# Layer 2's attention: exponentials one piece later, weighting ahead of scores, side work dealt by a piece's width, expert choice from an image's second chunk

## The chip, the core and the metric

The kernel runs on one core of a Trainium2 chip, as one program. The metric is the device time of one execution in microseconds (us). Before the change three runs took 7749.14, 7749.23 and 7750.11 us: the median is 7749.23.

The core's engines run their own queues in order: PE (TensorE; PEld is its weight load), DVE (VectorE), ACT (ScalarE), POOL (GpSimd) and SP, which issues the DMA transfers. They wait for each other by semaphores.

## What is computed

Four layers in a row act on an image batch of 4 x 56 x 56 x 128 in float32. Only layer 2 is touched. An image is seen there as 3136 tokens of 128 channels; first comes attention with additive scores, then a mixture of 64 experts in which each expert chooses 8 tokens:

```
h = x.shape[-1]
f = einsum('bih,ha->bia', x, W1[:h]);  g = einsum('bjh,ha->bja', x, W1[h:])      # 16 features
t = tanh(f[:, :, None, :] + g[:, None, :, :] + b1)
scores = einsum('bija,a->bij', t, w2[:, 0]) + b2[0]
e = exp(scores) * tril(ones, -1)                     # query i sees keys j < i
out = einsum('bij,bjh->bih', e / (sum(e) + 1e-10), x)
...
probs = softmax(x @ gate_w.T + gate_b, over tokens)  # each of 64 experts takes its 8 best tokens,
...                                                  # pools them, runs two matrix products with gelu
outputs.at[chosen tokens].add(expert output * its share)
```

Every pair of tokens (query after key) costs 16 tanh, and these are most of the layer's work.

## The kernel before, in words

**Pieces.** `layer2_attention` (L1007) cuts an image's 28 tiles of 112 tokens into four *chunks* of seven query tiles (784 queries). For chunk k, keys come in tiles J = 0 to 7(k + 1) - 1, and each key tile in two halves. A (chunk, J, half) is a *piece*; all four images make 560 of them (`pieces`, L1042 on). `span` (L1046) gives the queries that a piece needs: all 784 while J lies before the chunk, and in the chunk's last seven key tiles 784, 728, 672 and so on down to 56, as later keys are seen by fewer queries. The first kind is called *wide* here, the end of a chunk *narrow*. An image's first chunk has narrow pieces only.

**A piece's own work.** `adds` (L1157): seven VectorE adds of a query feature tile and a key scalar into a tile `th` (three buffers). `tangents` (L1169): one tanh over all seven on ScalarE. `scores` (L1175): 28 matmuls, or 14 where only one half of the columns is left, that sum the 16 features into a PSUM tile `s` (two buffers, one for both halves of a J). For each J then `weights` (L1196): one or two exponentials on ScalarE into `e` (two buffers), and in a chunk's last seven key tiles a triangular mask on GpSimd (L1208); and `weighted` (L1210): two or four matmuls of `e` and the keys into the PSUM tile `o` (one buffer per chunk).

**Order.** The stage is scheduled by hand: the order in which the Python loop (L1283 on) calls these functions is the order in each engine's queue. For piece i the loop calls the tanh of i; then `deal(0)`; then the adds of piece i + 2; the scores of i; after those, in a first half the exponential of the key tile before, in a second half its weighting; then `deal(1)`.

**Side work** is cut into small steps in four lists, and each `deal` (L1268) takes at most one step: from `urgent`, else from `now`, else (only in `deal(1)`) from `later_on`, else from `behind`. A step issues its instructions at once and can leave a rest (most often a copy out of PSUM on VectorE), which the next `deal` issues first. `urgent` and `now` get what a finished chunk needs (`attended`, L1223: two copies of `o`, then four `added` steps that divide and add to X) and the twelve steps that prepare the next chunk (`chunk_steps`, L1074: norm, transpose (`turn`), `by_group` with a GpSimd memset and eight DMA transfers into `xk`, `keys`, `queries`, each for four and for three tiles). `later_on` gets the next image's statistics and first chunk. `behind` gets the expert choice of the image before (`choose_steps`, L1388: statistics L1402, a square root through `rstd`, norms, transposes, logits, then over 3136 columns a maximum L1442, an exponential L1446, shares L1450, the best eight L1454 and their replacement L1459, then places and pooling), from J = 2 of each image's first chunk on; and in the last image the experts themselves for images 0 to 2 (`experts2_steps`, L1507: 32 weight loads of 1 MB, narrow, multiply, gelu; then per image a matrix by expert L1602, its copy L1610, and seven pairs of `scatter` L1616 and `scattered` L1622 that add to X). A step marked as holding the PSUM tile `m` keeps the other lists waiting for one deal.

Before the first adds of a chunk, `add_ahead` (L1258) runs whatever is left of `now` and `later_on` in line, each step with its rest at once. After the last piece, L1323 runs what is left of all lists in the same way, and only then does layer 3 (L1649) begin, with statistics of image 0 (L1828, L1829).

Of the kernel before, what the change touches and what calls it, by code (L numbers as in the profile page):

```python
# [18 lines left out]
B, HW, C = 4, 56, 128  # L19
S = HW * HW  # L20
P = 128
TP = 2 * HW
# [23 lines left out]

WT = 7
HALF = WT * TP // 2

E2, H2, K2 = 64, 512, 8  # L50
NHC = H2 // P
# [59 lines left out]
class Hybrid:  # L111
# [895 lines left out]
    def layer2_attention(self):  # L1007
# [5 lines left out]
        with ExitStack() as ctx:  # L1013
# [17 lines left out]
            pools = self.f2_wide, self.f2_sm, m, hold  # L1031
            root = lambda var: self.rstd(sm, var, [TP, NT], 1e-5, "ln", bufs=1)
# [4 lines left out]
            chunks = [(t, min(WT, NT - t)) for t in range(0, NT, WT)]  # L1037
            order = [(b, k) for b in range(B) for k in range(len(chunks))]


            pieces = [
                (j, J, half)  # L1042
                for j, (b, k) in enumerate(order) for J in range(sum(chunks[k])) for half in range(2)
            ]

            def span(j, J, half=0):  # L1046

                t, n = chunks[order[j][1]]
# [101 lines left out]
            def rounds(half):  # L1150

                return [
                    [(blk, 2 * half + q) for blk in range(3)] + ([(3, half)] if q == 0 else [])
                    for q in range(2)
                ]
# [13 lines left out]
            def tangents(i):  # L1169
                j, J, half = pieces[i]  # L1170
                lo, hi = span(j, J, half)
                own = th[i][:, :, lo:hi]
                nc.scalar.activation(own, own, AF.Tanh)  # L1173

            def scores(i):  # L1175
                j, J, half = pieces[i]
                if half == 0:
                    ps[j, J] = self.t(ps_s, [P, 2, 512], "s")
                z = th.pop(i)
                after = [h for h, _, _ in halves(*span(j, J, 1))]  # L1180
                at = 0
                for n, groups in enumerate(rounds(half)):
                    for h, lo, hi in halves(*span(j, J, half)):
                        for s, (blk, q) in enumerate(groups):
                            off = QW - JG - JG * q
                            rows = min(QW, TP - QW * blk)
                            nc.tensor.matmul(  # L1187
                                ps[j, J][QW * blk : QW * blk + rows, h, lo:hi],
                                place[:, off : off + rows],
                                z[:, at + s, h * HALF + lo : h * HALF + hi],  # L1190
                                start=(half == 0 and n == 0),
                                stop=(n == 1 or blk == 3) and (half == 1 or h not in after),
                            )
                    at += len(groups)

            def weights(j, J):  # L1196
                e = es[j, J] = self.t(sm, [TP, WT * TP], "e")
                s = ps.pop((j, J))[:TP, :, :HALF]
                lo = span(j, J)[0]
                if lo == 0:  # L1200
                    nc.scalar.activation(e.rearrange("p (h q) -> p h q", h=2), s, AF.Exp, bias=b2)  # L1201
                else:
                    for h, at, end in halves(*span(j, J)):
                        nc.scalar.activation(
                            e[:, h * HALF + at : h * HALF + end], s[:, h, at:end], AF.Exp, bias=b2
                        )
                if J >= chunks[order[j][1]][0]:
                    nc.gpsimd.tensor_mul(e[:, lo : lo + TP], e[:, lo : lo + TP], later)  # L1208

            def weighted(j, J):  # L1210
                b, k = order[j]
                t, n = chunks[k]
                if J == 0:
                    po[j] = self.t(ps_o, [P, 2, 512], "o")
                e = es.pop((j, J))
                for h, lo, hi in halves(*span(j, J)):
                    nc.tensor.matmul(  # L1217
                        po[j][:, h, lo:hi], xk[b, J // WT][:, J % WT, :],
                        e[:, h * HALF + lo : h * HALF + hi],
                        start=(J == 0), stop=(J == t + ((h + 1) * HALF - 1) // TP),  # L1220
                    )

            def attended(j):  # L1223
                b, k = order[j]
                t, n = chunks[k]
                oT = {}

                def copied(h):
                    if h == 0:
                        oT[0] = self.t(sm, [P, WT * TP], "oT", bufs=1)  # L1230
                    nc.vector.tensor_copy(oT[0][:, h * HALF : (h + 1) * HALF], po[j][:, h, :HALF])

                def added(s):
                    return self.attended_tiles(
                        b, t + s, min(2, n - s), oT[0][:, s * TP :], 1e-10, back, sm, ps_m, "m"
                    )

                return [bind(copied, h) for h in range(2)], [bind(added, s) for s in range(0, n, 2)]
# [11 lines left out]
                run(step)  # L1250
            weights2 = lambda: setattr(self, "w2", self.experts2_weights(self.f2_w, m))
            urgent, now, later_on, behind = [], [], [], []
            state = SimpleNamespace(held=False, after=lambda: None)
            first = {}
            for i, (j, J, _) in enumerate(pieces):
                first.setdefault(j, i)
# [1 line left out]
            def add_ahead(i):  # L1258
                if i < len(pieces):
                    j = pieces[i][0]  # L1260
                    if i == first[j] and j:
                        while now or later_on:
                            assert not state.held
                            run((now or later_on).pop(0))
                    adds(i)


            def deal(odd):  # L1268
                state.after()
                step = None  # L1270
                if urgent and not state.held:
                    step = urgent.pop(0)
                elif now and not state.held:
                    step = now.pop(0)
                elif later_on and odd and not state.held:
                    step = later_on.pop(0)
                elif behind:
                    step = behind.pop(0)
                    state.held = step.holds
                state.after = (step and step()) or (lambda: None)  # L1280

            add_ahead(0)
            add_ahead(1)  # L1283
            for i, (j, J, half) in enumerate(pieces):
                tangents(i)
                b, k = order[j]
                if half == 0 and J == 1 and k + 1 < len(chunks):
                    now += chunk_steps(j + 1)
                    if j == 0:
                        now.append(weights2)  # L1290
                if half == 0 and J == 8 and k + 1 == len(chunks) and b + 1 < B:
                    assert not behind
                    later_on += image_steps(b + 1) + chunk_steps(j + 1)
                if half == 0 and J == 2 and k == 0 and b:


                    behind += self.choose_steps(
                        b - 1, self.f2_pooled[:, :, b - 1], self.w2, pools, root
                    )
                    if b == B - 1:  # L1300
                        behind += self.experts2_steps(
                            range(B - 1), self.f2_pooled, self.w2, pools, 3, lambda: None
                        )
                deal(0)
                add_ahead(i + 2)
                scores(i)
                before = pieces[i - 2][:2] if i >= 2 else None
                if before and half == 0:
                    weights(*before)
                if before and half == 1:  # L1310
                    assert J != 1 or not urgent or j == 0
                    weighted(*before)
                    if before[0] != j:
                        copied, added = attended(before[0])
                        urgent += copied
                        now += added
                deal(1)
            state.after()
            j, J, _ = pieces[-1]
            weights(j, J)  # L1320
            weighted(j, J)
            copied, added = attended(j)
# [657 lines left out]
```

## Time and profile before

| | |
|---|---|
| median of three runs | 7749.23 us |
| the profiled execution | 7740.81 us |
| its span, first to last instruction | 7738.9 us |
| mean granted TensorE clock | 0.942 |
| busy over the span | PE 6639.4, DVE 6034.2, ACT 4865.4, POOL 2636.1 us |
| layer 2's attention, first to last tanh (L1173) | 3559.3 to 6192.5 us |
| tanh on ACT, L1173 | x560, 2181.6 us |
| adds on DVE, L1164 | x3920, 1866.2 us |
| scores on PE, L1187 | x14112, 1419.6 us |
| weighting on PE, L1217 | x1024, 390.7 us |
| exponentials on ACT, L1201 and L1204, in this stage | 167.8 and 63.1 us |
| mask on POOL, L1208 | x112, 144.1 us (half of them under 0.5 us each) |

How to read what follows. A row of a timeline has the start, the time from the first to the last of the instructions that it merges, the engine, line, operation, and what is written and read; in brackets stands how long the engine had been idle and who ended it. A wait row has who waited for whom, the sum in us, how often, and the longest. A row of the table by stages has a stretch of time and the busy time of each engine in it, with the number of instructions, then the granted clock (1.00 is full speed), the busy share of the DMA engines and GB/s. Matmul ends are modelled and spans on POOL are rough.

### The profile page before, as it was taken

The numbers are of one execution on the slowest core, as the hardware profiler recorded it, in microseconds if no ns is written. First come the engines' busy times: TensorE is split into PE (matmuls) and PEld (weight loads), VectorE is DVE, ScalarE is ACT, GpSimd is POOL, SyncE is SP. The second block draws the span as 40 slices with busy tenths as digits, with TensorE's granted clock in tenths as the row PEclk, the third lists the DMA queues.
The fourth block names the chain that finished last, engine by engine and source line by source line (L and its number), as shares of the span: only waits on it lengthen the run. The fifth ranks groups of instructions, "written<-read, shape, count | busy, mean of one in ns | idle before, by whom it ended". The sixth has DMA issues, their size and how long they took to land.

```text
span 7738.9 us, 105360 instructions
## 1 busy us (share of the span) xinstructions
PE 6639.4 (86%) x41289; PEld 2755.4 (36%) x41289; DVE 6034.2 (78%) x10279; ACT 4865.4 (63%) x4329; POOL 2636.1 (34%) x1938
## 2 busy tenths in 40 slices
PE   7888998999899899987777777777688889999999
PEld 3442333333333333323223332332233344454544
DVE  5786999999999999998787877888788754444434
ACT  4454556555655555556998899899899933333332
POOL 4555777777777777772001000100101100000000
PEclk9998999999999999998998999899899989999999
DMA  3000000000000000000000000000003201210000
GB/s 64 6 2 1 1 1 1 1 1 1 1 1 1 1 1 1 1 1 11 3 1 5 5 6 3 5 7 1 5 5 115 80 8 60 89 48 5 5 5 6
DMA packets 93641, 108.76 MB, mean 14 GB/s; under 512 B 24952, under 2 KB 56790, under 8 KB 92631
## 3 DMA queue, kind: packets, MB, share of 16 engines
q1 hardware_dynamic: 93143, 102.02, 4.6%
q8 instruction: 325, 5.32, 0.3%
q14 instruction: 173, 1.42, 0.1%
HBM read 85.28 MB, written 10.29 MB: 12 GB/s over the span
## 4 chain that ended last, share of the span: by engine, by line
PE 35%; DVE 34%; ACT 20%; issue 7%; POOL 2%; DVEq 0%; DMA 0%; SPq 0%; ACTq 0%; POOLq 0%
DVE hs L765 16%; ACT th L1173 12%; PE o L1761 7%; PE q L1750 7%; DVE u L758 6%; PE s L1187 5%; DVE th L1164 5%; PE pe L1915 2%; PE a L728 2%; DVE e L493 2%; ACT E L753 2%; PE m L894 2%; PE o L1217 1%; ACT e L1201 1%; DVE d L528 1%
## 5 line engine op out<-in xcount | busy, mean ns | idle before, releaser
L1173 ACT ACTIVATE th<-th 128x5488 f32<-128x5488 f32 (+13 forms) x560 | 2181.6, 3932 | 131.7 <-DVE th L1164 117.6
L770 POOL TENSOR_TENSOR hs<-hs,bc 128x896 f32<-128x896 f32 x896 | 1867.1, 2084 | 787.9 <-DVE hs L765 765.7
L1164 DVE TENSOR_SCALAR th<-fT,g 128x784 f32<-128x784 f32 (+13 forms) x3920 | 1866.2, 548 | 323.9 <-PE s L1187 271.1
L765 DVE TENSOR_TENSOR_SCAN hs<-E,u 128x896 f32<-128x896 f32 x896 | 1810.0, 2020 | 117.9 <-ACT E L753 2.0
L1187 PE MATMUL s<-th,place 128*32 128x392 f32 (+7 forms) x14112 | 1419.6, 497 | 489.2 <-ACT th L1173 487.4
L753 ACT ACTIVATE E<-a 128x896 f32<-128x896 f32 x896 | 821.5, 917 | 803.9 <-PE u L737 334.4
L728 PE MATMUL a<-delta,A_pick 32*128 32x448 f32 x3584 | 982.5, 600 | 143.8 <-ACT E L753 135.6
L758 DVE TENSOR_TENSOR u<-u,bc 128x896 f32<-128x896 f32 x896 | 964.1, 1076 | 60.0 <-PE u L737 59.5
L737 PE MATMUL u<-du,pick 32*128 32x448 f32 x3584 | 974.6, 600 | 35.2 <-DVE hs L765 35.2
L1187 PEld LDWEIGHTS s<-th,place 128*32 128x32 f32 (+1 forms) x14112 | 463.6, 113 | 1348.8 <-ACT th L1173 689.7
L1755 ACT ACTIVATE e<-q,shift 128x448 f32<-128x448 f32 (+1 forms) x700 | 441.4, 633 | 750.6 <-PE q L1750 750.4
L1761 PE MATMUL o<-e,xk 128*128 128x448 f32 (+1 forms) x1400 | 654.9, 550 | 25.7 <-ACT oT L1736 25.7
L1920 DVE SCALAR_TENSOR_TENSOR X<-pe,r_gate,X 112x128 f32<-112x128 f32 x896 | 314.1, 351 | 454.3 <-PE pe L1915 418.5
L1750 PE MATMUL q<-xT 128*128 128x448 f32 (+1 forms) x1400 | 654.0, 549 | 2.3 <-ACT e L1755 2.2
L728 PEld LDWEIGHTS a<-delta,A_pick 32*128 32x128 f32 x3584 | 295.4, 188 | 691.7 <-ACT E L753 467.7
L1208 POOL TENSOR_TENSOR e<-e,later 112x112 f32<-112x112 f32 x112 | 144.1, 1289 | 1140.2 <-ACT e L1201 658.9
L1217 PE MATMUL o<-e,xk 112*128 112x392 f32 (+5 forms) x1024 | 390.7, 501 | 75.1 <-POOL e L1208 75.1
L776 PE MATMUL y<-hs,sum 128*32 128x448 f32 x3584 | 446.4, 569 | 4.4 <-POOL hs L770 4.4
L1104 POOL MEMSET xa<- 112x4 f32 (+1 forms) x32 | 19.8, 619 | 1055.8 <-PE m L1097 1055.8
L1761 PEld LDWEIGHTS o<-e,xk 128*128 128x128 f32 (+1 forms) x1400 | 263.0, 192 | 310.5 <-issue 275.5
L737 PEld LDWEIGHTS u<-du,pick 32*128 32x128 f32 x3584 | 295.2, 188 | 197.6 <-DVE hs L765 181.5
L1750 PEld LDWEIGHTS q<-xT 128*128 128x128 f32 (+1 forms) x1400 | 248.9, 189 | 239.0 <-issue 213.8
(262 smaller groups left out, 7255.8 us busy)
## 6 DMA issues: line engine op xcount, KB each, us to landing
wide<-in_L_ffn_weight SPq DMA_DIRECT2D x64, 1024.0 KB
X<-in_x SPq DMA_DIRECT2D x8, 784.0 KB
out<-X SPq DMA_DIRECT2D x28, 224.0 KB
M<-wide SPq DMA_DIRECT2D x4, 784.0 KB
wide<-M SPq DMA_DIRECT2D x4, 784.0 KB
xk<-xa SPq DMA_DIRECT2D x96, 32.0 KB
xk<-xa SPq DMA_DIRECT2D x96, 24.0 KB
e_edge<-dtab SPq DMA_DIRECT2D x42, 49.0 KB
```

The source lines that it names most:

```text
L728: nc.tensor.matmul(halves(to)[:, k], w["A"][own, order[j][2], f, q, :], pre[j]["delta"][own, f], start=True, stop=True,)
L737: nc.tensor.matmul(halves(to)[:, k], w["pick"][own, q, :], pre[j]["du"][own, f], start=True, stop=True,)
L753: nc.scalar.activation(E[p + 1], t, AF.Exp)
L758: nc.vector.tensor_mul(v, v, pre[p // PAIRS]["bc"][:, 0:1].to_broadcast([P, 2, CH]))
L765: nc.vector.tensor_tensor_scan(flat, E.pop(p), V.pop(p), 0.0, op0=ALU.mult, op1=ALU.add)
L770: nc.gpsimd.tensor_mul(HS[p], HS[p], bc[:, 1:2].to_broadcast([P, 2, CH]))
L1164: nc.vector.tensor_scalar(th[i][:, s, lo:hi], fT[j][:, lo:hi], g[b, J // WT][:, at : at + 1], None, op0=ALU.add,)
L1173: nc.scalar.activation(own, own, AF.Tanh)
L1187: nc.tensor.matmul(ps[j, J][QW * blk : QW * blk + rows, h, lo:hi], place[:, off : off + rows], z[:, at + s, h * HALF + lo : h * HALF + hi] ...
L1217: nc.tensor.matmul(po[j][:, h, lo:hi], xk[b, J // WT][:, J % WT, :], e[:, h * HALF + lo : h * HALF + hi], start=(J == 0), stop=(J == t + ( ...
L1750: nc.tensor.matmul(ps[:n, :CH], xT[b][:, k : k + n], xT[b][:, c * CH : (c + 1) * CH], start=True, stop=True,)
L1761: nc.tensor.matmul(po[b, c], xk[b][:n, t, :], es.pop((b, c, t))[:n], start=(t == 0), stop=(t == N - 1))
```

## The change

Four things change, all in the loop of `layer2_attention`.

- **Exponentials.** The exponential of key tile J - 1 is issued after the scores of (J, second half), no longer after those of (J, first half): one piece later.
- **Weighting.** The weighting of key tile J - 2 is issued ahead of the scores of (J, first half); before, that of J - 1 came behind the scores of (J, second half). What follows a chunk's last weighting (`attended`) is put into the lists there too, its `added` steps at the head of `now`.
- **Dealing.** A piece earns 2.6 x (its width / 784), with at most 2 in hand; it may deal one step ahead of the adds for one in hand and a second at its end for two. A wide piece still deals two, a narrow one fewer. The rest of the first step now follows the scores of its own piece at the latest, and `later_on` is served by every other deal.
- **Choice.** `choose_steps` joins `behind` at J = 0 of the second chunk; for the last image it joins at J = 2 of the first, as before, with the experts.

```
+SHARE = 2.6
...
-            def deal(odd):
+            def deal():
                 state.after()
+                state.dealt += 1
...
-                elif later_on and odd and not state.held:
+                elif later_on and state.dealt % 2 and not state.held:
...
+            def gather(j, J):
+                weighted(j, J)
+                if J + 1 == sum(chunks[order[j][1]]):
+                    copied, added = attended(j)
+                    urgent.extend(copied)
+                    now[:0] = added
...
-                if half == 0 and J == 2 and k == 0 and b:
...
-                deal(0)
+                if b and half == 0 and (k, J) == ((0, 2) if b == B - 1 else (1, 0)):
+                    choose(b)
+                lo, hi = span(j, J, half)
+                state.credit = min(state.credit + SHARE * (hi - lo) / (WT * TP), 2)
+                may = [state.credit >= n for n in (1, 2)]
+                state.credit -= sum(may)
+                if may[0]:
+                    deal()
                 add_ahead(i + 2)
+                if i >= 4 and half == 0:
+                    gather(*pieces[i - 4][:2])
                 scores(i)
-                before = pieces[i - 2][:2] if i >= 2 else None
-                if before and half == 0:
-                    weights(*before)
-                if before and half == 1:
-                    assert J != 1 or not urgent or j == 0
-                    weighted(*before)
-                    if before[0] != j:
-                        copied, added = attended(before[0])
-                        urgent += copied
-                        now += added
-                deal(1)
+                state.after()
+                state.after = lambda: None
+                if i >= 3 and half == 1:
+                    weights(*pieces[i - 3][:2])
+                if may[1]:
+                    deal()
             state.after()
             j, J, _ = pieces[-1]
+            weighted(j, J - 1)
             weights(j, J)
             weighted(j, J)
```

(`choose(b)` holds the lines that put the choice and, for the last image, the experts into `behind`; they are the old ones.)

More of the change, by code (lines that the diff above doesn't have):

```diff
@@ L1252, in layer2_attention @@
             urgent, now, later_on, behind = [], [], [], []
-            state = SimpleNamespace(held=False, after=lambda: None)
+            state = SimpleNamespace(held=False, after=lambda: None, dealt=0, credit=0)
             first = {}
@@ L1280, in deal, with choose @@
                 state.after = (step and step()) or (lambda: None)
+            def gather(j, J):
[4 more added lines that the diff above has]
+                    now[:0] = added
+            def choose(b):
+                behind.extend(self.choose_steps(
+                    b - 1, self.f2_pooled[:, :, b - 1], self.w2, pools, root
+                ))
+                if b == B - 1:
+                    behind.extend(self.experts2_steps(
+                        range(B - 1), self.f2_pooled, self.w2, pools, 3, lambda: None
+                    ))
             add_ahead(0)
@@ L1293, in layer2_attention @@
                     later_on += image_steps(b + 1) + chunk_steps(j + 1)
-                if half == 0 and J == 2 and k == 0 and b:
[L1297 to L1303, printed above, removed]
-                deal(0)
+                if b and half == 0 and (k, J) == ((0, 2) if b == B - 1 else (1, 0)):
[6 more added lines that the diff above has]
+                    deal()
                 add_ahead(i + 2)
+                if i >= 4 and half == 0:
+                    gather(*pieces[i - 4][:2])
                 scores(i)
-                before = pieces[i - 2][:2] if i >= 2 else None
-                if before and half == 0:
-                    weights(*before)
-                if before and half == 1:
-                    assert J != 1 or not urgent or j == 0
-                    weighted(*before)
-                    if before[0] != j:
-                        copied, added = attended(before[0])
-                        urgent += copied
-                        now += added
-                deal(1)
+                state.after()
[4 more added lines that the diff above has]
+                    deal()
             state.after()
             j, J, _ = pieces[-1]
+            weighted(j, J - 1)
             weights(j, J)
```

## The prediction

> **What bounds the kernel now.** The change touches layer 2's attention alone, so I first looked for its stage: the groups of instructions put the 560 tanh of L1173 between 3559.3 and 6192.5 us, and the per-stage table by chunks shows who fills it.
>
> ```profile
> 3609.90:3725.60 115.70, 90.17 (x791) 36.59 (x791) 97.11 (x227) 111.45 (x45) 10.82 (x9) 0.95 0.02 5
> 4189.30:4250.90 61.60, 41.60 (x375) 20.46 (x375) 48.55 (x161) 41.26 (x24) 11.70 (x10) 0.83 0.03 8
> 4250.90:4395.10 144.20, 105.03 (x839) 43.24 (x839) 121.65 (x292) 124.46 (x65) 5.09 (x9) 0.89 0.02 4
> 4395.10:4587.90 192.80, 155.68 (x1291) 64.10 (x1291) 161.67 (x360) 184.95 (x74) 8.89 (x9) 0.93 0.03 7
> 6192.50:6225.70 33.20, 20.35 (x122) 15.95 (x112) 12.43 (x31) 0.64 (x3) 0.42 (x1) 0.65 0.16 35
> ```
>
> Columns after the stretch: its length, then busy time of PE, PEld, DVE, ACT and POOL. ScalarE (ACT) fills almost all of a chunk: 111.45 of 115.70 in image 0's second chunk, 184.95 of 192.80 in image 1's third. Where it does not, VectorE is as busy: image 1's first two chunks have 41.26 and 124.46 ACT against 48.55 and 121.65 DVE in 61.60 and 144.20. Length minus ACT busy, over all 16 chunks: first chunks 10.2, 20.3, 19.4, 19.5 (sum 69.4), second 4.3, 19.7, 20.2, 20.1 (64.3), third 10.1, 7.8, 6.3, 8.6 (32.8), fourth 13.4, 15.3, 12.4, 7.2 (48.3): **214.8 us of ACT idle is all that can be won in the stage.** Behind it stands a tail of 33.2 us with ACT empty.
>
> ACT's waits in this stage say what the idle is made of:
>
> ```profile
> ACT th L1173 <- DVE th L1164: 117.6, 65, 6.4
> ACT e L1201 <- PE s L1187: 26.2, 19, 2.7
> ACT e L1204 <- PE s L1187: 19.0, 18, 2.6
> ACT th L1173 <- DVE den L1335: 13.0, 11, 1.8
> ```
>
> 45.2 us are exponentials waiting for scores; 117.6 are tanh waiting for VectorE's adds. The ACT timeline at the end of image 1's first chunk shows the worst place, short tanh starved by dealt-out VectorE work, then a square root whose input is last in that queue:
>
> ```profile
> 4243.99 0.53 ACT L1173 ACTIVATE th<-th 128x392 f32<-128x392 f32 x1 [3.20 <-DVE th L1164]
> 4250.93 4.78 ACT L1173 ACTIVATE th<-th 128x5488 f32<-128x5488 f32 x1 [6.41 <-DVE th L1164]
> 4263.43 0.23 ACT L155 ACTIVATE ln_r<-ln_ve 112x28 f32<-112x28 f32 x1 [6.18 <-DVE ln_ve L153]
> ```
>
> At other chunk ends POOL's mask L1208, usually 0.5 us, lasts 11.6, and PE stands behind it (POOL and PE timelines, image 0):
>
> ```profile
> 3912.52 0.52 POOL L1208 TENSOR_TENSOR e<-e,later 112x112 f32<-112x112 f32 x1 [3.08 <-ACT e L1204]
> 3915.03 11.99 POOL L1208 TENSOR_TENSOR e<-e,later 112x112 f32<-112x112 f32 x2 [2.00 <-ACT e L1204]
> 3926.70 1.11 PE L1217 MATMUL o<-e,xk 112*128 112x224 f32 x2 [10.55 <-POOL e L1208]
> ```
>
> VectorE runs three full-width groups of adds without a gap from 3913.88 to 3926.37; the mask ends when they do. I call this the **mask stall**.
>
> **Part by part.** No arithmetic is added or removed; instructions move in PE, ACT, DVE, POOL and SP order.
>
> *Exponentials and weighting.* At a plain chunk start (image 0, fourth chunk) the old order takes 35.6 us from the tanh of J0 first half (3918.93) to that of J3 (3954.50). New order: the mask of the last-but-one tile still arrives inside the wide adds, and its weighting still stands before J0's scores, so the adds of J1's second half still start 14.05 after the first tanh (3932.98) and end at 17.9. ACT, done with three tanh and a small exponential at 14.3, waits 3.6 for them: the price of a mask stall. From there it runs three tanh of 4.67 and two exponentials of 0.91 unbroken: 33.8. VectorE needs 3 x 3.8 for adds, 1.05 for two copies and 3 x 1.0 for additions in that time, 15.5 of 15.9, so it just keeps up. Gain 1.8; where a chunk ends, the exponential now falls into the 3.2 us wait of the next chunk's first tanh, another 0.4. The new wait is PE's for exponential and mask ahead of scores; queued behind it are those scores, for which adds three pieces on wait. In wide pieces exponential plus mask (0.9 + 0.5) end 3 us before that piece's tanh. Fourth chunks: three at 10.5, and the last image's at 4 (its scatters leave it, a mask stall comes): 35.5 for 48.3, **gain 13**.
>
> *Dealing by width.* Counting the loop, an image's chunks have 17, 45, 73 and 101 slots in place of 28, 56, 84 and 112. In first chunks of images 1 to 3 the 18 steps of attended and next chunk no longer fit: five (last norm, turn, by_group, keys, queries) are run in line before the second chunk's first adds. That ladder: 0.35 norm, 0.8 transposes, 0.50 copy, 1.8 keys, 0.26, 0.9 queries, 0.50 copy, 3.84 adds and seven hops of 0.2 = 10.4, some 0.8 beside the last short tanh: 9.6 idle. With 3.5 of mask stall, 2.4 where VectorE is behind with the four additions, 1.5 of small ones: 17 each for 19.7; image 0 7 for 10.2. Sum 58, **gain 11**. by_group's POOL memset and its eight xk DMAs go with the ladder; xk is first read seven key tiles later, and a transfer took 1.98 in the chain, so I cost them nothing; uncovered they would add 2 each.
>
> *Choice from the second chunk.* Its 28 statistics pairs (0.45 each, 12.6) leave the narrow pieces for wide ones, where ACT's 10.4 a pair of pieces leaves VectorE 2.7. The chunk starts on 7.2 of them plus attended, so ACT loses about 4; the root waits 2.5 (the same helper in fourth chunks: 1.6 to 1.95, plus a late exponential) in place of 6.18; the end is like image 0's, 4: 10.5 for 20. Image 0 3.5. Sum 35, **gain 29**. But largest (3.40), shares (1.85), eight and replaced (3.4 each) go on into the third chunk, and the narrow pieces before it, now free of steps, get the mask stall as image 0 has it: 3.7 stall, 2.4 behind largest, 1.6 c_MT as now, 3.0 boundary, 1.3 others: 12 for 7.6, three times; image 0 7. Sum 43, **loss 10**. The unseen costs here lie between none (in the first two chunks VectorE keeps 48.55 + 121.65 less some 15.2 of steps that leave, 155, for ACT's 41.3 + 124.3 less 3.1, 162.5) and all of these steps exposed (12.6 + 12.1 an image); I take the middle, nearer the rows of image 0.
>
> *The tail.* The last image has 44 slots fewer, five of them made good in line: the list left at the end grows from 21 steps to 61. Three images' scatters instead of one and a bit then run one after another with ACT empty:
>
> ```profile
> 6197.53 1.12 PE L1616 MATMUL m<-c_oe,wide 64*112 64x128 f32 x8 [0.35 <-ACT c_oe L1610]
> 6199.44 1.12 PE L1616 MATMUL m<-c_oe,wide 64*112 64x128 f32 x8 [0.79 <-DVE X L1622]
> 6210.78 2.04 PE L1616 MATMUL m<-c_oe,wide 64*112 64x128 f32 x8 [0.78 <-DVE X L1622]
> 6213.61 2.04 PE L1616 MATMUL m<-c_oe,wide 64*112 64x128 f32 x8 [0.79 <-DVE X L1622]
> 6227.55 1.28 ACT L1834 ACT_TABLE_LOAD   x1 [30.07 <-DVE lc_mv L1829]
> ```
>
> A scatter and its add take 1.91 from start to start, and 2.83 once the granted clock has gone from 1.00 to 0.50. Nine pairs start after the last tanh now, 21 will: 12 x 2.83 + 2 x 1.0 for the hops to the next image = **loss 36**; at the high clock 25. The reloads of M were 5 us each from issue to quiet, and two are issued before the tail, the third 20 us ahead of its use; uncovered, 5.
>
> One rule of the Trainium skill speaks against the slow price: "TensorE: Matmul & The Clock Gate", HAM oscillation, has the clock fall after idle gaps over about 3.4 us, and PE's gaps here are 0.8. By the page the tail would cost 25; by the row the clock stood at 0.87 in 6200 to 6203 and 0.50 after, with no longer gap ahead of it.
>
> Another, "SBUF — State Buffer", Who interferes with whom, lets a blocked GpSimd instruction in after the one VectorE instruction that holds the port; by the page a mask would wait 0.5, and the new stalls of the third chunks would not come. The row has it waiting behind 21 wide adds.
>
> **Sum.** 13 + 11 + 29 - 10 = 43 won, 36 lost: 7 less. The profiled execution took 7740.8 (span 7738.9, 1.9 around it); that gives 7733.8. It lies 8.4 under the median 7749.2 of the three runs, and I carry that: **7742**. The measurement can hardly tell 0.2% (15.5 us) from nothing, so this forecast is "no change" by that measure.
>
> **Rivals.** (1) *The mask stalls dissolve.* If the later exponential makes masks run before or after the wide adds, eleven chunk starts lose their 3.6: 40 less, 7702, and 7691 with the tail at the high clock. For it: image 1's second chunk ends with masks of 0.42. Against: those had VectorE steps between the adds, and the new order has none. (2) *Weighting ahead of scores stalls the narrow pieces.* At a chunk's last pairs, exponential 0.55, mask 0.5, weighting 1.15, scores 0.9 and adds 1.0 with hops make 4.6 against ACT's 4.9. From a mask of about 0.8 on, scores, adds and tanh slide. Masks of 2.2 and 2.6 stand in the trace (3573.36, 3615.00); two pieces in 15 chunk ends at 1.2 lose 36: 7778, **slower**. Against: ACT's idle there is under 0.1 now, and most masks last 0.5. (3) *The exponentials' 45 us turn into tanh waits*, because VectorE is behind anyway, the rest of the gain pays for the tail, and nothing moves: 7749.
>
> **Chances.** Forecast 0.46 (own range 7725 to 7760: of it 0.14 faster by over 0.2%, 0.29 within, 0.03 slower), rival 1 0.25 (faster), rival 2 0.22 (slower), rival 3 0.07 (within). Faster 0.39, within 0.36, slower 0.25. The range reaches to rival 1 and rival 2: 7700 to 7778.
>
> **What would show it.** ACT's waits for PE in L1201 and L1204 near 2; the 6.18 before the root near 2; 9 to 10 ahead of the second chunks' first tanh; a mask of 11 us at every later chunk end, those of images 1 to 3 included; some 70 us, not 33, between the last tanh and layer 3's first statistics, most of it in 2.83 steps. I am wrong if ACT's idle in the stage falls to under 140 or stays over 195, or if the tail is under 55.

## The result, and the profile after

The changed kernel takes **7736.18 us** (median of 14 runs, 7730.31 to 7748.95) against 7745.61 of the kernel before in the same sessions (14 runs, 7728.79 to 7751.61): a ratio of 0.9993 with a 95% interval of 0.9985 to 1.0001 (it is taken over all runs; the two medians alone give 0.9988). By this measurement that is no change. The forecast was 7742, and 3.6 of the 5.8 us between them are the kernel before, for which three runs had given 7749.23. The profiled execution took 7735.35 us, with a span of 7732.8.

"No change" hides two large movements, each near its forecast. The stage from first to last tanh went from 2633.2 to 2586.0 us: 47.2 won, 43 forecast. The tail, from the last tanh to layer 3's first statistics, went from 33.1 to 71.8: 38.7 lost, 36 forecast. (Layer 2 also began 3.7 us later in this run; nothing before it was edited.)

The per-stage table of the changed kernel, with the stretches that the prediction showed: image 0's second chunk, image 1's first three, the tail. Columns after the length: busy time of PE, PEld, DVE, ACT and POOL, then the granted clock.

```profile
3609.20:3729.90 120.70, 91.44 (x793) 36.80 (x793) 97.35 (x227) 111.36 (x45) 20.10 (x10) 0.93 0.02 4
4184.60:4241.00 56.40, 40.73 (x375) 20.37 (x375) 43.48 (x129) 40.54 (x25) 16.20 (x10) 0.88 0.04 8
4241.00:4373.30 132.30, 105.87 (x835) 41.94 (x835) 115.67 (x317) 120.55 (x62) 11.23 (x9) 0.91 0.02 4
4373.30:4573.20 199.90, 154.98 (x1295) 63.47 (x1295) 173.44 (x367) 187.77 (x76) 12.38 (x9) 0.95 0.03 7
6149.10:6220.90 71.80, 50.32 (x226) 41.02 (x225) 20.21 (x42) 1.43 (x5) 0.84 (x2) 0.54 0.17 38
```

Image 1's first two chunks became 5 and 12 us shorter, its third 7 us longer, and VectorE's work went the same way (43.48 for 48.55, 115.67 for 121.65, 173.44 for 161.67). Image 0's second chunk, with no choice in it, became 5 us *longer*. In the tail the clock is 0.54.

ACT's waits in the stage:

```profile
ACT th L1174 <- DVE th L1165: 144.1, 68, 8.0
ACT th L1174 <- DVE den L1349: 19.2, 15, 4.0
ACT th L1174 <- PE o L1218: 4.4, 6, 0.7
ACT ln_r L156 <- DVE ln_ve L154: 2.6, 3, 0.9
```

Of the 45.2 us of exponentials waiting for scores 0.6 is left; the root's waits of about 6 are 0.9 at most. Waits for adds rose from 117.6 to 144.1. The two worst places come next. First ACT and DVE at the end of image 1's first chunk, and the steps run in line that they wait for:

```profile
4232.09 0.53 ACT L1174 ACTIVATE th<-th 128x392 f32<-128x392 f32 x1 [1.51 <-DVE th L1165]
4233.20 2.00 PE L1121 MATMUL m<-xT,wg 128*128 128x42 f32 x16 [0.60 <-DVE xT L1101]
4235.55 0.83 PE L1139 MATMUL m<-xT,wf 128*128 128x336 f32 x2 [0.35 <-DVE g L1129]
4237.04 7.62 DVE L1165 TENSOR_SCALAR th<-fT,g 128x784 f32<-128x784 f32 x14
4240.98 9.45 ACT L1174 ACTIVATE th<-th 128x5488 f32<-128x5488 f32 x2 [8.03 <-DVE th L1165]
```

Keys, queries and the adds stand one behind the other, and the second chunk's first tanh waits 8.03: the in-line ladder, in each of images 1 to 3.

Second the mask stall, at the start of image 0's fourth chunk:

```profile
3915.62 12.67 DVE L1165 TENSOR_SCALAR th<-fT,g 128x56 f32<-128x56 f32 x28 [0.64 <-ACT e L1205]
3915.71 0.45 POOL L1209 TENSOR_TENSOR e<-e,later 112x112 f32<-112x112 f32 x1 [2.36 <-ACT e L1205]
...
3918.07 10.51 POOL L1209 TENSOR_TENSOR e<-e,later 112x112 f32<-112x112 f32 x1 [1.91 <-ACT e L1205]
3920.86 9.45 ACT L1174 ACTIVATE th<-th 128x5488 f32<-128x5488 f32 x2 [2.87 <-DVE th L1165]
3928.63 1.11 PE L1218 MATMUL o<-e,xk 112*128 112x224 f32 x2 [10.53 <-POOL e L1209]
3929.67 6.91 PE L1188 MATMUL s<-th,place 128*32 128x392 f32 x56
...
3934.09 7.62 DVE L1165 TENSOR_SCALAR th<-fT,g 128x784 f32<-128x784 f32 x14 [5.80 <-PE s L1188]
...
3938.06 4.78 ACT L1174 ACTIVATE th<-th 128x5488 f32<-128x5488 f32 x1 [2.85 <-DVE th L1165]
```

Read it as a chain: the mask of 3915.71 takes 0.45 beside the first seven of the 28 adds, of 56 columns each; the next one, beside the 21 of 784, takes 10.51 and ends as they end. PE stands 10.53 behind it, because this weighting is ahead of the next scores, as it was before the change (10.55 there); VectorE, with all three `th` buffers full, stands 5.80 behind the scores; ACT loses 2.85. Nine chunk ends show a mask of 9.9 to 10.5 us.

### The profile page after: what moved, and what is told of

Same layout as the page of the kernel before. It is cut to its first block, busy times and chain, and to the rows that moved or that the text cites. A ratio compares the mean times of both kernels' runs of the same rounds, so it can differ in the third digit from the quotient of the medians.

```text
span 7732.8 us, 105420 instructions
## 1 busy us (share of the span) xinstructions
PE 6629.6 (86%) x41289; PEld 2749.0 (36%) x41289; DVE 6040.2 (78%) x10279; ACT 4856.7 (63%) x4329; POOL 2690.5 (35%) x1938
## 5 line engine op out<-in xcount | busy, mean ns | idle before, releaser
L1174 ACT ACTIVATE th<-th 128x5488 f32<-128x5488 f32 (+13 forms) x560 | 2184.2, 3945 | 170.2 <-DVE th L1165 144.1
L766 DVE TENSOR_TENSOR_SCAN hs<-E,u 128x896 f32<-128x896 f32 x896 | 1810.0, 2020 | 117.6 <-ACT E L754 1.9
L1188 PE MATMUL s<-th,place 128*32 128x392 f32 (+5 forms) x14112 | 1390.3, 489 | 440.8 <-ACT th L1174 438.2
L1209 POOL TENSOR_TENSOR e<-e,later 112x112 f32<-112x112 f32 x112 | 162.6, 1452 | 1078.6 <-ACT e L1202 656.9
L1105 POOL MEMSET xa<- 112x4 f32 (+1 forms) x32 | 55.1, 1723 | 970.2 <-PE m L1098 970.2
```

What stands on the lines that cost most here:

```text
L766: nc.vector.tensor_tensor_scan(flat, E.pop(p), V.pop(p), 0.0, op0=ALU.mult, op1=ALU.add)
L1188: nc.tensor.matmul(ps[j, J][QW * blk : QW * blk + rows, h, lo:hi], place[:, off : off + rows], z[:, at + s, h * HALF + lo : h * HALF + hi] ...
```

## The experiments

Time is the median, the ratio that to the kernel before in the same session with its 95% interval. Stage and tail, measured as above, come from one profiled execution each. Where the code of the stage is the same, it took 2586.0, 2586.0 and 2586.2 in three kernels, but 2542.6 and 2538.3 in the last two, and image 1, with the same code, 8 us more in `mask_tail_last` than in `mask_on_tensor`. So a difference of less than some 8 us between two stages tells little by itself.

| kernel | us | ratio | stage | tail |
|---|---|---|---|---|
| before | 7735.92 to 7746.25 by session | 1 | 2633.2 | 33.1 |
| changed | 7736.18 | 0.9993 [0.9985, 1.0001] | 2586.0 | 71.8 |
| order_alone | 7722.86 | 0.9974 [0.9963, 0.9984] | 2611.7 | 37.1 |
| dealing_alone | 7777.02 | 1.0045 [1.0030, 1.0060] | 2630.5 | 71.4 |
| choice_alone | 7729.72 | 0.9984 [0.9975, 0.9993] | 2618.7 | 33.2 |
| order_and_choice | 7716.02 | 0.9963 [0.9949, 0.9977] | 2602.3 | 37.5 |
| last_image_two | 7706.88 | 0.9948 [0.9932, 0.9965] | 2594.2 | 37.1 |
| mask_on_tensor | 7707.63 | 0.9954 [0.9939, 0.9969] | 2552.8 | 71.6 |
| tail_two_buffers | 7712.03 | 0.9959 [0.9946, 0.9973] | 2586.0 | 47.4 |
| tail_all_rows | 7699.23 (one run) | | 2586.2 | 38.0 |
| all_three | 7686.06 | 0.9924 [0.9911, 0.9936] | 2576.5 | 31.0 |
| mask_tail_last | 7674.20 | 0.9915 [0.9900, 0.9930] | 2572.1 | 30.7 |
| second_chunk_ahead | 7651.91 | 0.9887 [0.9870, 0.9903] | 2542.6 | 31.0 |
| ahead_all_rows | 7642.25 | 0.9879 [0.9863, 0.9896] | 2538.3 | 30.3 |

### One part at a time

`order_alone` is the changed kernel with `may = [True, True]` (two steps in every piece) and the choice at J = 2 of the first chunk.

> The exponentials a piece later and the weighting ahead of scores, alone: two steps are dealt in every piece and the choice joins at J = 2 of the first chunk, as in the kernel before. My theory: the 45.2 us that exponentials wait for scores fall under 3, fourth chunks lose 10 to 13 us together, and the stage from first to last tanh goes from 2633 to 2613 - 2620; the tail stays at 33. Rival (the exponentials' waits turn into tanh waits): stage within 5 us of 2633, tanh waits for adds 117.6 to 150 or more. Rival (weighting ahead of scores stalls narrow pieces full of steps): stage over 2645.

Stage 2611.7: my theory's side, 21.5 won. The exponentials' waits are gone, and the tanh waits are 165.6, as the rival wanted. Both are true: ACT waits 48 us longer for adds, but within the stage no longer for scores (43.0 of the 45.2 us stood there), and three waits ahead of the root come to 2.6 us for 18.5. Fourth chunks win 20.7 together, for the 10 to 13 expected; first chunks lose 6.3. The tail is 4 longer than I expected, with 22 steps left instead of 21.

`dealing_alone` is the kernel before with the dealing by width alone (credit, `may`, and the rest of a first step issued behind the scores of its piece).

> Dealing by width alone, in the old order of exponentials and weighting; the choice joins at J = 2 of the first chunk. As behind is served last and a first chunk has 17 slots for 18 other steps, the choice falls to the second chunk by itself. My theory now: this one edit carries what the prediction booked under dealing and under choice: the second chunks of images 1 to 3 go from 144 to about 136, first chunks from 61 to 57, third chunks up by 5 each, stage 2633 to 2600 - 2612, tail 72. Exponential waits stay near 45. Rival (as the prediction booked it): 11 us of stage from dealing, the rest from the choice, stage 2618 - 2625.

Both theories fell: stage 2630.5, only 2.7 won. By kind of chunk, it wins 16 in first chunks and 26 in second ones, and loses 35 in third ones, where I had put 5 each, and 4 in fourth ones. The largest new wait comes from PE's queue, not VectorE's: 16.7 us in three places. POOL, PE and ACT of this kernel at the end of image 1's second chunk:

```profile
4381.65 11.82 POOL L1209 TENSOR_TENSOR e<-e,later 112x112 f32<-112x112 f32 x2 [2.68 <-ACT e L1205]
4393.14 1.11 PE L1218 MATMUL o<-e,xk 112*128 112x224 f32 x2 [10.54 <-POOL e L1209]
4394.19 1.76 PE L1440 MATMUL h<-c_xT,gwT 128*64 128x448 f32 x2
4395.98 0.63 ACT L1445 ACTIVATE wide<-h,gb 64x448 f32<-64x448 f32 x1 [5.58 <-PE h L1440]
```

The mask is held again, the choice's logits stand behind it in PE's queue, and ACT's queue, in order, waits 5.58 with the bias for the logits. In the changed kernel the mask there takes 0.42 to 0.83 and this wait does not exist: the new order and the dealing are worth 24.2 apart and 47.2 together.

`choice_alone` is the kernel before with the choice at `(k, J) == (1, 0)`, the last image apart.

> The choice from the second chunk alone (last image as before), old order, two steps dealt in every piece. My theory: the statistics leave the narrow pieces of images 1 and 2's first chunks (3 to 5 us less each) and the root's 6.2 us wait in the second chunk falls to about 2; image 3, whose choice stays, shows nothing. Stage 2633 to 2618 - 2626, tail 33. Rival (VectorE is behind there anyway, and the choice's steps only move the wait): stage within 5 us of 2633.

Stage 2618.7, in the range; 14.4 won. First chunks win 14.1 (images 1 and 2 some 6 to 7 each, for 3 to 5), and what the other chunks win and lose cancels. But in the changed kernel this edit does **nothing**: with the choice put back to J = 2 of the first chunk there, the program comes out the same, instruction for instruction. A first chunk deals 17 steps, 18 others are served before `behind`, and so the choice begins in the second chunk wherever it is queued. What the prediction booked as "choice from the second chunk" is an effect of the dealing.

`order_and_choice` is the changed kernel without dealing by width (`may = [True, True]`).

> The changed kernel without the dealing by width: two steps in every piece, as before the change; order of exponentials and weighting new, choice from the second chunk (last image as before). By the runs of one part alone, order won 21.5 us of stage and choice 14.4. Theory A (parts add up; dealing by width gives the stage nothing once choice has moved, and costs the tail): stage 2633 - 36 = 2597, tail 37, some 7705 in all, 30 under the changed kernel. Theory B (dealing frees the narrow pieces for the new order, as the changed kernel's stage is 25 shorter than that of the new order alone): stage over 2605 here, total 7715 or more. First chunks of images 1 and 2 under 56.4 (no ladder in line) would be for A.

Stage 2602.3, between the theories; the first chunks of images 1 and 2 take 57.7 and 61.5, over the 56.4 that would be for A. Once order and choice are in, dealing by width wins 16 us of stage and costs 34 of tail: without it the kernel is 20 us faster than the changed one.

### The tail's price

`last_image_two`: two steps a piece in the last image alone.

```
+                if b == B - 1:
+                    may = [True, True]
```

> The changed kernel, but in the last image every piece deals two steps as before the change, so that 22 steps and not 61 are left for the end. My theory: the tail goes from 71.9 to 33 - 36, and the last image's first, second and third chunk give back 5 to 12 us of the stage (2586 to 2591 - 2598): some 28 us faster than the changed kernel, span about 7705. Rival (the steps cost as much in narrow pieces as in the tail): stage over 2615, no gain.

Near enough: tail 37.1, stage 8.2 back, 7706.88. Most of what the changed kernel won and lost again lies in this one place.

`tail_two_buffers`: in the list left at the end, scatters write `m` and `h` in turn.

```
+            def either():
+                turns.n += turns.tail
+                return hold() if turns.n % 2 else m()
...
-            pools = self.f2_wide, self.f2_sm, m, hold
+            pools = self.f2_wide, self.f2_sm, either, hold
```

> The changed kernel, but the scatters left at the end take two PSUM tiles in turn, so that PE need not wait for VectorE's addition of the one before. Theory (21 pairs of 2.83 us: 2.04 PE, 0.05 hop, 0.69 VectorE, 0.05 hop, at half clock): pairs fall to PE's 2.0 - 2.1, tail 72 to 54 - 58. Rival (the clock halves because of the gaps of 0.78 us between scatters): with the gaps gone the granted clock returns to 1.00, pairs of 1.12 - 1.2, tail 36 - 40. Nothing in the stage.

Tail 47.4: under the theory's 54 and over the rival's 40, so both missed the size. The first seven scatters start 0.96 apart, the rest 1.71 apart. The per-stage table, and PE's timeline:

```profile
6152.00:6156.00 4.00, 4.00 (x36) 3.78 (x35) 2.95 (x5) 0.00 (x0) 0.00 (x0) 1.00 0.78 193
6156.00:6160.00 4.00, 2.87 (x23) 2.32 (x22) 2.32 (x4) 0.26 (x1) 0.00 (x0) 1.00 0.67 132
6160.00:6164.00 4.00, 4.00 (x21) 4.00 (x21) 2.20 (x4) 0.00 (x0) 0.00 (x0) 0.50 0.68 146
6164.00:6168.00 4.00, 4.00 (x20) 4.00 (x20) 1.56 (x3) 0.00 (x0) 0.00 (x0) 0.50 0.00 0
```

```profile
6164.16 1.91 PE L1637 MATMUL h<-c_oe,wide 64*112 64x128 f32 x8
6165.87 1.91 PE L1637 MATMUL m<-c_oe,wide 64*112 64x128 f32 x8
```

The clock falls at the end of the second row, in which PE pauses between two images and is busy 2.87 of 4 us. Then PE is busy 4.00 of 4 us, and the granted clock stays at 0.50: gaps between scatters are not what keeps it halved. (So the fall itself did not come while PE was busy 4.00 of 4, as the next expectation puts it.) What the scatters have that the attention's other matmuls do not is a contraction over 64 rows (64*112, against 128*32 for scores and 112*128 for weighting). `tail_all_rows` changes that, with M in both halves of the tile and zeros as the other operand's lower half:

```
+            nc.sync.dma_start(out=r["M"][E2:], in_=w["M"][images[i]])
...
+            nc.gpsimd.memset(r["oe", i][E2:], 0.0)
```

> The changed kernel with two PSUM tiles in the tail, and each scatter's contraction over 128 rows in place of 64: M is loaded into both halves of the tile and the lower half of the expert outputs is zero, so the sums are the same. In the run with two PSUM tiles the granted clock fell to 0.50 some 10 us after the stage though PE was busy 4.00 of 4 us, so gaps are not what halves it. Theory (the clock goes by how much of the array the matmuls use): clock 1.00 to the end of the scatters, 0.96 a pair, tail 47 to 31 - 35. Rival (the clock goes by something that ends with the attention, whatever PE does): 0.50 from some 10 us on, tail 45 - 50.

```profile
6160.00:6164.00 4.00, 3.14 (x26) 2.58 (x24) 2.35 (x4) 0.04 (x1) 0.20 (x1) 1.00 0.22 45
6164.00:6168.00 4.00, 3.69 (x32) 3.60 (x32) 2.02 (x3) 0.22 (x1) 0.00 (x0) 1.00 0.95 213
6176.00:6180.00 4.00, 3.40 (x30) 3.08 (x29) 3.45 (x6) 0.00 (x0) 0.00 (x0) 1.00 0.02 5
6184.00:6188.00 4.00, 1.62 (x8) 1.16 (x7) 1.87 (x8) 0.00 (x0) 0.00 (x0) 0.53 0.00 0
```

The first row has the same pause between two images, 3.14 of 4 us busy, and the clock does not fall. It stays at 1.00 through all 21 scatters, though PE is mostly *less* busy than above, and falls only when 1.5 to 1.6 of 4 us are used. Scatters start 0.96 apart. The tail is 38.0 and not 31 to 35; of the 3 us over the range, 2.5 are PE's waits of 1.29 and 1.19 for M's transfer. This is one execution; `ahead_all_rows` below is a second.

### The mask stall's price

`mask_on_tensor`: no mask on GpSimd; instead, after a key tile's first-half scores, an identity matmul adds a tile of 0 and -10000 to the scores, so that masked exponentials become zero.

```
...
+                        nc.tensor.matmul(
+                            ps[j, J][:TP, h, at:end], self.ident[:TP, :TP],
+                            later[:, from_ : from_ + end - at],
+                            start=False, stop=h not in after,
+                        )
...
-                    nc.gpsimd.tensor_mul(e[:, lo : lo + TP], e[:, lo : lo + TP], later)
```

> The changed kernel, but the triangular mask is a matmul that adds -10000 to the scores in PSUM in front of the exponential (identity times a constant tile, one or two a key tile, 112 key tiles), and GpSimd has no mask any more. Theory (the 10.5 us masks behind VectorE's wide adds hold PE's weighting, scores and so the adds and tanh three pieces on): the nine chunk ends lose their stall of 2.4 to 3.7 us ahead of the tanh of (J = 1, second half), the first chunks of images 1 to 3 the 1.65 ahead of J = 4: stage 2586 to 2552 - 2562; PE's mask matmuls cost under 0.5 each in narrow pieces where PE has room. Rival (VectorE is behind there anyway): the waits stay over 2 in the same places, stage over 2575.

Stage 2552.8, 33.2 won: the theory holds for the nine chunk ends. It does not for the first chunks: the 1.65 ahead of J = 4 is still there in images 1 to 3, and the ladder has grown from 8.03 to 9.0 to 9.7. Fourth chunks become 17.8 shorter together, and two of four are left with 0.3 us of ACT idle in their wide pieces. The chunk start shown above, now:

```profile
3914.74 12.49 DVE L1165 TENSOR_SCALAR th<-fT,g 128x56 f32<-128x56 f32 x28 [0.56 <-PE s L1188]
...
3917.55 0.65 PE L1226 MATMUL o<-e,xk 112*128 112x224 f32 x2
3919.80 9.45 ACT L1174 ACTIVATE th<-th 128x5488 f32<-128x5488 f32 x2 [2.87 <-DVE th L1165]
3924.63 8.09 PE L1188 MATMUL s<-th,place 128*32 128x392 f32 x56 [6.43 <-ACT th L1174]
3929.15 0.34 ACT L1215 ACTIVATE e<-s,b 112x112 f32<-112x112 f32 x1
3929.39 9.57 ACT L1174 ACTIVATE th<-th 128x5488 f32<-128x5488 f32 x2
```

The weighting no longer waits, scores start when the tanh is done, and the third and fourth tanh run as one unbroken pair. The 2.87 in front of the first tanh is still there: it is the wide adds themselves, and the mask has no part in it.

### Putting it together

`all_three`: order, choice, mask on TensorE and the two tail buffers, without dealing by width.

> New order and choice from the second chunk, two steps in every piece (no dealing by width), mask added on TensorE, two PSUM tiles in the tail. If the parts add up: stage some 2597 - 25 = 2572, tail 32 - 35, 7676 to 7684 in all. If narrow pieces full of steps keep the stalls: stage over 2585.

7686.06, 2 above the range; stage 2576.5, 4 over the sum and 24 over `mask_on_tensor`. So with the masks gone dealing by width is worth 24 us of stage in these profiles, for 16 with them; 8 us more is what single executions differ by, and that it grew is not shown.

`mask_tail_last`: the changed kernel with its dealing, plus mask on TensorE, two tail buffers and two steps a piece in the last image.

> The changed kernel with dealing by width kept, plus mask added on TensorE, two PSUM tiles in the tail, and two steps a piece in the last image. If the three add up: stage 2552.8 + 8.2 = 2561, tail 31, in all 7707.6 - 71.6 + 31 + 8 = 7675. If two steps a piece cost more once the mask is off GpSimd (the run with all pieces at two steps lost 24 us of stage), 7683 or more.

The time, 7674.20, is the theory's; the profiled execution (7683.75, the slowest of its runs) shows the rival's stage, 2572.1. Of the 19 us over `mask_on_tensor`, 11.8 are the last image's, and 7.9 stand in image 1, whose program is the same. There a wait of 2.4 ahead of the tanh of (J = 6, second half) is 5.7. The granted clock makes it: the same weighting and scores on PE a little ahead of that tanh, and the per-stage rows, in `mask_on_tensor` and then in `mask_tail_last`:

```profile
4295.74 1.56 PE L1226 MATMUL o<-e,xk 112*128 112x392 f32 x4
4297.23 2.83 PE L1188 MATMUL s<-th,place 128*32 128x392 f32 x28
4296.00:4299.00 3.00, 3.00 (x26) 1.14 (x28) 1.81 (x5) 3.00 (x2) 0.00 (x0) 1.00 0.15 35
```

```profile
4295.73 2.96 PE L1232 MATMUL o<-e,xk 112*128 112x392 f32 x4
4298.62 4.53 PE L1194 MATMUL s<-th,place 128*32 128x392 f32 x28
4296.00:4299.00 3.00, 3.00 (x8) 1.07 (x11) 1.57 (x4) 3.00 (x2) 0.00 (x0) 0.50 0.13 29
```

The query copy on VectorE waits for a matmul behind these scores, the adds stand behind the copy and four pairs of statistics, and the tanh waits for the adds. In images 1 and 2 of this kernel, of `mask_on_tensor`, `second_chunk_ahead` and `ahead_all_rows`, the wait is 2.4 where the clock holds, 4.0 where it is 0.50 for 3.4 us and 5.7 where it is for 6.8 us. Another 1.7 us comes the same way in image 1's third chunk (a tanh waits 2.67 for 0.98, with the clock at 0.50 in 4398 to 4401). Why the clock falls at this place in one execution and not in another stays open.

`second_chunk_ahead` goes for the ladder (8.03 and 9.07 in images 2 and 1 of the run before, up to 9.7 in `mask_on_tensor`): the second chunk's preparation is queued in the fourth chunk of the image before, and two steps a piece begin with the last image's second chunk.

```
-                    later_on += image_steps(b + 1) + chunk_steps(j + 1)
+                    later_on += image_steps(b + 1) + chunk_steps(j + 1) + chunk_steps(j + 2)
...
-                elif later_on and state.dealt % 2 and not state.held:
+                elif later_on and state.dealt % 4 and not state.held:
...
-                if half == 0 and J == 1 and k + 1 < len(chunks):
+                if half == 0 and J == 1 and k + 1 < len(chunks) and (k or not b):
```

> As the run before, with two steps a piece only from the last image's second chunk on, and the preparation of images 1 to 3's second chunk dealt in the fourth chunk of the image before (three of four deals go to that list; three buffers for the query features; room for them by letting the second layer's spread inputs share the hidden layer's buffer). Theory (the 8 to 9.3 us ahead of the second chunk's first tanh are the five steps run in line): that wait falls to 2.9, first chunks of images 1 to 3 from 54.6 to 45 - 48, fourth chunks of images 0 to 2 lose 0 to 4 each: stage 2561 to 2536 - 2545, 7650 to 7662 in all. Rival (VectorE is the bound there, and the steps cost the fourth chunks what the first ones win): stage over 2555.

ACT at the end of image 1's first chunk in this kernel:

```profile
4216.74 0.53 ACT L1180 ACTIVATE th<-th 128x392 f32<-128x392 f32 x1 [0.66 <-DVE th L1171]
4217.18 0.43 ACT L1221 ACTIVATE e<-s,b 112x224 f32<-112x224 f32 x1
4220.48 4.78 ACT L1180 ACTIVATE th<-th 128x5488 f32<-128x5488 f32 x1 [2.87 <-DVE th L1171]
```

The 8.03 of the changed kernel has become 2.87, the first chunks of images 1 and 2 take 45.6 and 45.3 (image 3's, with the choice in it, 53.2, a miss), and the fourth chunks before them pay nothing (259.3, 259.2). 7651.91, and the theory holds in all but that.

`ahead_all_rows` adds the 128-row scatters to it.

> The run with the second chunk's preparation ahead, plus the scatters' contraction over 128 rows. In that run the clock is 0.50 through the seven scatters after the last tanh: they start 1.71 us apart, and stood 0.96 apart with all rows. Theory: clock 1.00 to the last scatter, seven times 0.75 us less and 2 on the last weightings: tail 31.0 to 24 - 26, stage as it was (2540 - 2546), some 6 us less in all. Rival (the second transfer of M, 0.8 MB, ends later than the clock wins): tail 29 - 32.

The clock is 1.00 through five of the seven scatters, but the tail is 30.3: the rival's number, though not for its reason. PE and DVE in the tail:

```profile
6113.77 1.13 PE L1652 MATMUL m<-c_oe,wide 128*112 128x128 f32 x8
6118.95 2.05 PE L1652 MATMUL h<-c_oe,wide 128*112 128x128 f32 x8 [4.04 <-DVE X L1658]
```

```profile
6117.07 1.22 DVE L1704 TENSOR_TENSOR ew<-ew,ew_last 128x1024 f32<-128x1024 f32 x1 [3.35 <-DMA ew_last<-in_L_ffn_expert_w]
6118.21 0.68 DVE L1658 TENSOR_TENSOR X<-h,X 112x512 f32<-112x512 f32 x1
```

VectorE's queue holds a layer 3 addition that waits for its weights' transfer, and the scatters' additions stand behind it. The transfer ended no later than before (this addition began at 6118.20 in `second_chunk_ahead`); the scatters only came to it earlier, PE idled 4.04, and the clock then fell to 0.50. At 0.9879 [0.9863, 0.9896] this is the best version, not told apart from the one before it; its wins over both the old and the changed kernel are far outside the noise.

## Why the prediction came out, point by point

- **The bound.** ACT waiting on VectorE and PE, 214.8 us of idle: right. 176.7 are left, 38 fewer, where 43 were forecast. The stage won 9 more than that, since ACT instructions that follow without a break overlap: their single durations, 12 us more in sum than before, exceed the time they cover by 107 us, and by 86 before.
- **Exponentials and weighting (gain 13 in fourth chunks).** Measured 17.6 of idle there (48.3 to 30.7), 20.7 of length in the run of this part alone. Three chunks stand at 7.5 to 8.5 for the 10.5 forecast, the last at 6.8 for 4. Right in mechanism, and the mask stall was kept in the sum, as it should: it costs 2.4 to 3.7 at a time.
- **Dealing by width (first chunks, gain 11).** 15.7 (69.4 to 53.7). The ladder of five steps was right in its steps and 8.03 for 9.6 in size.
- **Choice from the second chunk (gain 29, loss 10).** Here the prediction failed twice, and was saved by other terms. The steps do move to the second chunk, but the dealing moves them; the edit itself is without effect. And second chunks won 15.4, not 29: left with 48.9 us of idle for "3.5 + 3 x 10.5". Image 0's went from 4.3 to 9.3, because its first chunk, rid of steps, got a mask stall that I had not listed; those of images 1 to 3 keep 11.7 to 14.4, among it 2.9 to 5.7 in front of J = 6's second half, where the last statistics are dealt and the granted clock is 0.50 for 3.4 to 6.8 us just before. The root's wait did fall from 6.18 to 0.9, but it falls as far in the run of the order alone and in that of the dealing alone (three waits of 18.5 in sum come to 2.6 and 2.7), so it is no gain of the choice. Third chunks lost 10.6 for 10, in part by luck. I had masks of 11 us there too; at the ends of the second chunks they took 0.42 to 0.83, and what waits instead is a tanh for `den`, 3.95 and 3.50 in images 1 and 2, where the clock is 0.50 for 6.8 us ahead of it; in image 3, where it is not, 0.97. The sum had the clock's falls in the tail alone, and no term for those in the stage.
- **The tail (loss 36).** 38.7, in 2.83 steps as costed. I had the right price without its reason. By the Trainium skill's page "TensorE: Matmul & The Clock Gate", HAM oscillation, which has the clock fall at gaps over about 3.4 us, it would have been 25 (an estimate). The measurement decides: the clock was 0.50 with gaps of 0.78 between scatters, and it stayed 0.50 with none. With 128 rows in the contraction in place of 64 it stayed at 1.00 (`tail_all_rows`, one execution, and five scatters of `ahead_all_rows`).
- **Rival 1 (the mask stalls dissolve, 40 less).** It did not happen. `mask_on_tensor` shows that its price was near: 33 for 40.
- **Rival 2 (weighting ahead of scores stalls narrow pieces).** A new wait on `o` of 0.73 shows at six places, 4.4 us in all, against the 36 it needed.
- **Rival 3 (the exponentials' 45 us turn into tanh waits).** In part: tanh waits for adds rose 26.5. The stage fell nevertheless.

The sum came out because errors cancelled: second chunks 14 too good; first and fourth chunks 9 too bad, the overlap 9 unlisted, the tail 3 too good.

## What to carry to other kernels

Count what a changed dealing rule leaves for the end as carefully as what it frees in the middle: 40 steps moved to where nothing hides them took back four fifths of it. Before pricing an edit to a queue with priorities, follow the queue: an entry moved in a list that is not served has no price at all. And parts that meet in one in-order queue don't add: here 24 apart, 47 together.

## What the runs showed of the hardware

- GpSimd's mask, 0.42 us when free, is held for 9.9 to 11.6 us by a train of 21 VectorE adds of 784 columns, until the train ends, and gets by seven adds of 56 columns in 0.45. The Trainium skill's page "SBUF — State Buffer", in Who interferes with whom, has the blocked engine wait for the instruction that holds the port; the traces here show it held through all that were left.
- With f32 matmuls that contract 64 rows TensorE's granted clock held at 1.00 through the first seven scatters, fell to 0.50 at a pause between two images (PE busy 2.87 of 4 us) and stayed there through nearly unbroken work (3.60 to 4.00 of 4, 6160 to 6184 us of `tail_two_buffers`). With 128 rows it stayed at 1.00 over the same pause and with less busy time (3.1 to 4.0 of 4). With 128 rows it fell in an idle gap of 4.04 us.
- In the stage too the granted clock falls to 0.50, for 3.4 us or a multiple of it, and not at the same places in each execution: at one place with the same code a tanh waits 2.4, 4.0 or 5.7 us, by whether the clock fell for none, 3.4 or 6.8 us ahead of it.
